# The order in which two engines read a group's score banks, one table for Exp and Ln, and the order of the first and last turns, in a two-layer cross-attention kernel

## The chip, the cores and the metric

The kernel runs on one core of a Trainium2 chip, entirely in fp32. The metric is the device time of one execution in microseconds (us), as the median of several executions. The engines are named as in the profile: PE (matrix multiplies), DVE (VectorE), ACT (ScalarE), POOL (GpSimd), and SP, whose queue issues nearly all the DMAs. "L77" is line 77 of the kernel.

## The reference, cut to what matters

Two cross-attention layers follow each other on x of 4 x 512 x 320; both read the same context of 4 x 1024 x 512, and both have 20 heads of 16 and four image tokens ("ip") at the end of the context. Layer 0 also fuses a second score into the ip attention: the text probabilities times the *context itself* (512 columns), normalised to length one and multiplied with the normalised ip tokens.

```python
def layer0(x, ctx):
    text, ip = ctx[:, :-4], ctx[:, -4:]
    probs = softmax(q @ k_text.T * D**-0.5)                      # per head, 512 x 1020
    text_out = probs @ v_text
    qsem = l2norm(probs @ text)                                  # per head, 512 x 512
    sem = qsem @ l2norm(ip).T
    probs_ip = softmax(q @ k_ip.T * D**-0.5 + 0.5 * sem) * spatial_mask
    return (text_out + probs_ip @ v_ip) @ W_out + b_out + x

def layer1(x, ctx):
    text, ip = ctx[:, :77], ctx[:, 77:]                          # ip: the other 947 rows
    out = softmax(q @ k_text.T * D**-0.5) @ v_text + softmax(q @ k_ip.T * D**-0.5) @ v_ip
    return out @ Wo.T + bo + x
```

## The kernel before, in words

**Work and loops.** A turn is one batch and one block of 128 queries: 16 turns. A turn has five groups of four heads, so there are 80 groups `gi` in one long loop, and each group is two `Unit`s (pairs of heads). A `Unit` has four parts (`part0` to `part3`), in which PE makes layer 0's large products of probabilities and context (tiles named `b`). After every part comes a `stop`, numbered k = 0 to 7 within the group. A stop takes one item from a queue (`sub`, else `late`, else `proj`, which holds the next batch's projections), then does what the loop's rules add to it:

```python
        item()
        if k < 2:
            fill0(gi + 1, k)
        if k in (2, 4, 5, 6) or ending[0] and k < 2 or gi >= len(G) - HG and k == 7:
            l1_step()
```

**The scores of the next group.** `fill0(gi + 1, k)` calls `fill` (L464), for the context half c = k. PE writes 32 small products `sc` into two PSUM tiles of two banks each, two heads to a tile; the heads alternate, so that the first two products need tile 0 and the third already needs tile 1. For each tile in turn, ACT copies it to `e` (L476) and DVE takes the maximum over the blocks of the half (`m`, L477; the profile gives it the line of the helper, L87). The tiles come from the pool `ps_sc`, which holds just two of them. The next half's `sc` therefore take the same two tiles, and so do layer 1's score products: `mx` (scores for the maximum, in `do_max`) and `ex` (the same scores less the maximum, for Exp, in `do_exp`).

**Layer 1.** It runs one turn late, in `l1_step`s. A step makes `mx` of group g + 1, takes the rows' maxima on DVE, and then makes `ex` of group g, whose Exp is on ACT. After four steps of a group, `do_pv` multiplies with the values, and `normalise` divides on DVE and POOL. A turn is `linked` if at least four steps of the turn before are still queued: its maxima then ride on those steps, instead of having two steps of their own (`first_maxima`).

**The end of a turn of layer 0.** `finish(turn)` (L831) is emitted after the turn's fifth group. It works on small tiles of 128 x 20 to 128 x 320: the reciprocal of the sums, the squared lengths `n2`, a `Sqrt` on ACT (L857) and a reciprocal for 1/length, then the ip softmax with an `Exp` on ACT (L866) and the spatial mask. These are the scheduler's to place. Two empty items, `turn_ip`, `add_ip`, `turn_out` and `multiply` follow in the queue `late`, and `multiply` starts layer 1 of the turn.

**Order.** `mm`, `tr` and `vec` keep PE's instructions and those of DVE issued through `vec` in program order; the plain `nc.vector` operations of `finish`, and ACT, POOL and most DMAs, are ordered by a scheduler. [...]

**PSUM.** `ps_sc` has 2 x 2 banks, `ps_qs` three single banks for the `b` products, and `ps_tp` one bank (`tp`) for transposes, projections and `pv`. When the large products are not running (`idle`), `tp` also hands out the three `qs` banks.

**Start and end of the program.** At the start the context of batch 0 is transposed in four quarters (`turns`, tiles `cT`); behind each quarter's transposes come `sums`, DVE combinations of the raw context that are sent to DRAM (`td`) for later products. Then come keys (`keys0`, `last_k`), queries (`q0`) and values (`v0`), whose weights `load_w` brings through two buffers. At the end, after the last group, a loop takes an item and a layer-1 step by turns until nothing is left; there turn 15's layer 0 is finished, and its whole layer 1 runs.

Of the kernel before, what the change touches and what calls it, by code (L numbers as in the profile page):

```python
# [13 lines left out]
F32 = mybir.dt.float32  # L14
AF = mybir.ActivationFunctionType
# [40 lines left out]
def xattn_pair(ctx_stack: ExitStack, tc: tile.TileContext, a: dict, out: bass.AP):  # L56
    nc = tc.nc

    def pool(name, bufs, **kw):
        return ctx_stack.enter_context(tc.tile_pool(name=name, bufs=bufs, **kw))  # L60

    cst = pool("cst", 1)
    big = pool("big", 1)
    wts = pool("wts", 2)
    ep = pool("ep", 8)
    e1p = pool("e1p", 6)
    st2 = pool("st2", 2)
# [25 lines left out]

    ending = [False]
    idle = [True]
    turn_of = [0]

    def tp(name):
        turn_of[0] += 1
        if idle[0] and turn_of[0] % 4:  # L100
            return ps_qs.tile([P, 512], F32, tag=f"qs{turn_of[0] % 4 - 1}", name=name)
        return ps_tp.tile([P, 512], F32, tag="tp", name=name)
# [8 lines left out]
            nc.scalar.copy(o, i)  # L111


    ident = cst.tile([P, P], F32, name="ident")
    make_identity(nc, ident)

# [28 lines left out]
    recent = []  # L145

    def load_w(b, *names):

        for k, t in recent:
            if k == (b, names):  # L150
                return t
        t = wts.tile([P, EC, C + NIP], F32, tag="w", name=f"{'_'.join(names)}_{b}_{len(recent)}_{turn_of[0]}")
# [8 lines left out]
        recent.append(((b, names), t))  # L161
        del recent[:-2]
        return t


# [42 lines left out]
    def normalised_ip():  # L208
        ipraw = st2.tile([B * NIP, E], F32, tag="pc", name="ipraw")
        for b in range(B):  # L210
            nc.scalar.dma_start(ipraw[b * NIP : (b + 1) * NIP, :], a["ctx_2048"][b, NTXT0:T, :])
        ipsq = st2.tile([B * NIP, E], F32, tag="pc", name="ipsq")
        ipn = cst.tile([B * NIP, 1], F32, name="ipn")
        nc.scalar.activation(ipsq, ipraw, AF.Square, accum_out=ipn)
        nc.vector.tensor_scalar(ipn, ipn, EPS2, None, ALU.max)
        ipl = cst.tile([B * NIP, 1], F32, name="ipl")
        nc.scalar.activation(ipl, ipn, AF.Sqrt)
        ipr = cst.tile([B * NIP, 1], F32, name="ipr")
        nc.vector.reciprocal(ipr, ipl)
        nc.vector.tensor_scalar(ipsq, ipraw, ipr, None, ALU.mult)  # L220
        pt = tp("pt_ipn")
        for e in range(EC):
            tr(pt[:, e * 16 : (e + 1) * 16], ipsq[:, e * P : (e + 1) * P], ident[:16, :16])
        nc.vector.tensor_copy(ipnT.rearrange("p e n -> p (e n)"), pt[:, 0 : EC * 16])
# [50 lines left out]
    def projections(b):  # L275
# [9 lines left out]
        z.loads = []  # L285

        def quarter(n):

# [130 lines left out]
            return [[lambda: turn(0), lambda: (turn(1), sums())], [lambda: keys(0)], [last_keys],  # L419
                    [lambda: values0(0), lambda: values0(1)], [values_ip] if n == 3 else [], [lambda: keys(1)], v1]  # L420

        def query_steps(s):
# [41 lines left out]
    def fill(c, m, name):  # L464


        ps = [ps_sc.tile([P, 2, 512], F32, tag="sc", name=f"sc{name}_{c}_{i}") for i in range(2)]
        for j in range(TH):
            t = (TH * c + j) * P
            for r in range(4):  # L470
                mm(ps[r // 2][:, r % 2, j * P : (j + 1) * P], kq[0][0][32 * r : 32 * r + D, t : t + P],
                   qq[0][0][32 * r : 32 * r + D, :], True, True)
        e = []
        for i in range(2):
            e.append(ep.tile([P, 2, TH, P], F32, tag="e0", name=f"e{name}_{c}_{i}"))
            nc.scalar.copy(e[i].rearrange("p h t s -> p (h t s)"), ps[i].rearrange("p h n -> p (h n)"))  # L476
            vec.tensor_reduce(m[:, c, 2 * i : 2 * i + 2, :],  # L477
                                    ps[i][:, :, 0 : (TH - c) * P].rearrange("p h (t s) -> p h s t", s=P), AX.X, ALU.max)
        return e


# [1 line left out]
    def layer1(turn):  # L483
# [5 lines left out]
        def name_of(g):  # L489
            return f"1_{turn}_{g}"  # L490

        def do_max(g, i, half):

            if g not in ms:
                ms[g] = st2.tile([P, 2, 4], F32, tag="m1", name=f"m{name_of(g)}")
            k, m = buffer(1, turn, g), ms[g][:, :, 2 * i : 2 * i + 2]
            ps = ps_sc.tile([P, 2, 512], F32, tag="sc", name=f"mx{name_of(g)}_{i}_{half}")
            for j in range(2):
                r = 32 * (2 * i + j)
                mm(ps[:, j, :], qq[1][k][r : r + D, :], kq[1][k][r : r + D, half * 512 : half * 512 + 512], True, True)  # L500
# [4 lines left out]
            if half == 0:  # L505
                vec.tensor_reduce(rows(R_TXT), ps[:, :, 0:NTXT1], AX.X, ALU.max, negate=True)
            vec.tensor_reduce(m[:, half, :], ps[:, :, 0 if half else NTXT1 : 512], AX.X, ALU.max, negate=True)
            if half:
                vec.tensor_tensor(rows(R_IP), m[:, 0, :], m[:, 1, :], ALU.min)

        def do_sub(g):

            k = buffer(1, turn, g)
            pt = tp(f"pt_nm{name_of(g)}")
            tr(pt[:, 0:P], nmz[k], ident)
            qas[g] = st2.tile([P, P], F32, tag="qa", name=f"qa{name_of(g)}")
            vec.tensor_tensor(qas[g], pt[:, 0:P], qq[1][k], ALU.add)
# [78 lines left out]
        def step(g, k):  # L596
# [8 lines left out]
            nxt = after(1)  # L605
            if nxt and (g + 1 < HG or nxt[0].linked):
                nxt[0].do_max(nxt[1], 1 - x, half)
            if sub:
                sub.popleft()()
            do_exp(g, x, half)  # L610
# [220 lines left out]
    def finish(turn):  # L831
# [6 lines left out]
        def wide(t, n=NIP):  # L838
            return t.unsqueeze(2).to_broadcast([P, H, n])
# [5 lines left out]
        nc.vector.reciprocal(r, pv[:, :, V0W - 1])  # L845
        o = small("o", [P, H, D])
        nc.vector.tensor_tensor(o, pv[:, :, 0:D], wide(r, D), ALU.mult)
        sem = small("sem", [P, H, NIP])
        nc.vector.tensor_tensor(sem, pv[:, :, D : D + NIP], wide(r), ALU.mult)

        n2 = small("n2", [P, H])
        nc.vector.tensor_tensor(n2, ss[:, :, 0], ss[:, :, 1], ALU.add)
        nc.vector.tensor_tensor(n2, n2, r, ALU.mult)
        nc.vector.tensor_tensor(n2, n2, r, ALU.mult)
        nc.vector.tensor_scalar(n2, n2, EPS2, None, ALU.max)
        n1 = small("n1", [P, H])
        nc.scalar.activation(n1, n2, AF.Sqrt)  # L857
        rn = small("rn", [P, H])
        nc.vector.reciprocal(rn, n1)
        nc.vector.tensor_tensor(sem, sem, wide(rn), ALU.mult)  # L860
        pe = small("pe", [P, H, NIP])
        nc.vector.scalar_tensor_tensor(pe, sem, SEM_SCALE, ips, ALU.mult, ALU.add)
        mx = small("mx", [P, H])
        nc.vector.tensor_reduce(mx, pe, AX.X, ALU.max)
        nc.vector.tensor_tensor(pe, pe, wide(mx), ALU.subtract)
        nc.scalar.activation(pe, pe, AF.Exp)  # L866
        sums = small("sums", [P, H])
        nc.vector.tensor_reduce(sums, pe, AX.X, ALU.add)
        re = small("re", [P, H])
        nc.vector.reciprocal(re, sums)  # L870
        nc.vector.tensor_scalar(re, re, spat[:, s : s + 1], None, ALU.mult)
        nc.vector.tensor_tensor(pe, pe, wide(re), ALU.mult)
        of2, box = o.rearrange("p h d -> p (h d)"), {}

        def turn_ip():
# [22 lines left out]
            vec.tensor_tensor(xr[:, 0, :], pt[:, 0:C], xr[:, 0, :], ALU.add)  # L898
            layer1(turn)


        late.extend([lambda: None] * 2 + [turn_ip, add_ip, turn_out, multiply])


    z, (turns, keys0, last_k, v0, vip, keys1, v1, q0) = projections(0)
# [12 lines left out]

    run(keys0[3:])
    load_w(0, "L0_xattn_W_k", "L1_xattn_Wk")  # L920
    run(keys0[:3])
    run(q0[:4])
    run(last_k)
    load_quad(0, z, 0, 0)
    run(v0[:2])
    load_w(0, "L0_xattn_W_v_ip")
# [57 lines left out]
    for gi, (turn, g) in enumerate(G):  # L984
# [49 lines left out]
```

## Time and profile before

| what | value |
|---|---|
| median of 3 runs (lowest, highest) | 3739.45 us (3739.18, 3739.75) |
| the profiled execution's own time | 3740.82 us |
| its span | 3739.0 us |
| mean granted PE clock | 0.961 |
| busy: PE, DVE, ACT, POOL | 94%, 56%, 40%, 27% |
| PE busy in the first 100 us, and from 3600 us to the end | 65.77 of 100.00; 89.32 of 139.00 |

The span is the time between the first and the last recorded instruction; the execution's time is 1.8 us longer. PEclk is the share of full clock that PE was granted. The row of a group of instructions gives busy time and the mean of one; the idle time of that engine just before them stands behind, with what ended it.

### The profile page before, as it was taken

What the parts mean: (1) busy time and instruction counts of PE and PEld (TensorE: products, weight loads), DVE (VectorE), ACT (ScalarE), POOL (GpSimd) and SP (SyncE); (2) the same over time, 40 slices, a digit from 0 to 9 for tenths busy, and PEclk for the clock granted to TensorE, in tenths of its full rate; (3) what the DMA queues carried; (4) which work ended last, traced back from release to release, by engine and by line L of the source; (5) the groups of instructions that cost most, each with busy time, mean ns of one, the idle gap of its engine ahead of it and who ended that gap; (6) DMA issues with size and microseconds to landing.
All of it is one profiled execution on the core that took longest, in us unless ns stands there. A gap on an engine that the chain in (4) does not pass through costs nothing.

```text
span 3739.0 us, 74161 instructions
## 1 busy us (share of the span) xinstructions
PE 3529.3 (94%) x29060; PEld 2812.8 (75%) x29060; DVE 2083.0 (56%) x3794; ACT 1500.1 (40%) x2824; POOL 1015.8 (27%) x1040
## 2 busy tenths in 40 slices
PE   6999999999999999999999999999999999999976
PEld 5777777777788777877777787777777777777765
DVE  2344555665655654666564555556656666665543
ACT  1333344444443433444443433444444444444432
POOL 2222222322232222232232222223223323322210
PEclk8999999999999999999999999999999999999986
DMA  6354332222344243222324334222232222222211
GB/s 193 103 133 113 89 72 39 43 40 53 78 95 114 59 98 87 53 51 42 70 65 111 90 90 100 46 58 40 48 82 44 43 44 51 41 46 38 45 35 26
DMA packets 704987, 258.76 MB, mean 69 GB/s; under 512 B 571024, under 2 KB 679024, under 8 KB 704640
## 3 DMA queue, kind: packets, MB, share of 16 engines
q1 hardware_dynamic: 704464, 253.82, 30.1%
q8 instruction: 232, 3.80, 0.4%
q14 instruction: 115, 0.94, 0.1%
q10 hardware_dynamic: 176, 0.20, 0.0%
HBM read 213.51 MB, written 40.33 MB: 68 GB/s over the span
## 4 chain that ended last, share of the span: by engine, by line
PE 80%; DVE 11%; ACT 3%; issue 2%; DMA 2%; SPq 1%; POOL 0%; ACTq 0%; POOLq 0%; DVEq 0%
PE b L77 48%; PE ex L77 6%; PE pv L77 5%; DVE m L87 4%; PE sc L77 4%; PE pt_k L77 4%; DVE e L87 4%; PE mx L77 4%; PE pt_v L77 4%; PE pt_y L77 2%; PE pt_q L77 2%; PE mx L92 1%; ACT e L710 1%; ACT e L476 1%; ACT junk L790 1%
## 5 line engine op out<-in xcount | busy, mean ns | idle before, releaser
L77 PE MATMUL b<-xv_t,e 128*128 128x277 f32 x2560 | 669.8, 404 | 0.5 <-DVE c L87 0.4
L77 PE MATMUL b<-xv,e 128*128 128x277 f32 (+1 forms) x2560 | 652.6, 407 | 2.7 <-ACT e L710 2.7
L77 PEld LDWEIGHTS b<-xv,e 128*128 128x128 f32 x2560 | 479.4, 190 | 136.9 <-ACT e L710 3.2
L77 PEld LDWEIGHTS b<-xv_t,e 128*128 128x128 f32 x2560 | 482.2, 193 | 113.6 <-DVE c L87 3.1
L710 ACT ACTIVATE e<-e 128x1024 f32<-128x1024 f32 x320 | 338.3, 1057 | 456.0 <-DVE e L87 455.7
L805 POOL TENSOR_TENSOR e<-e,s 128x512 f32<-128x512 f32 x160 | 224.2, 1401 | 1081.1 <-PE b L77 1081.1
L87 DVE TENSOR_REDUCE m<-sc 128x256 f32<-128x1024 f32 (+1 forms) x320 | 338.1, 1088 | 282.9 <-ACT e L476 282.9
L529 ACT ACTIVATE e<-ex 128x1024 f32<-128x1024 f32 x320 | 326.0, 1019 | 236.7 <-PE ex L77 236.6
L87 DVE TENSOR_REDUCE m<-mx 128x2 f32<-128x870 f32 (+1 forms) x320 | 363.8, 1137 | 96.9 <-PE ex L77 90.6
L790 ACT ACTIVATE junk<-c 128x256 f32<-128x256 f32 x480 | 198.7, 414 | 486.4 <-DVE c L87 478.5
L77 PE MATMUL ex<-qa,kq 19*128 19x128 f32 x5120 | 383.3, 290 | 6.8 <-DVE qa L87 5.9
L77 PE MATMUL mx<-kq,qq 16*128 16x512 f32 x1280 | 365.3, 661 | 21.5 <-DVE m L87 15.6
L476 ACT COPY e<-sc 128x1024 f32<-128x1024 f32 x320 | 307.5, 1012 | 193.5 <-PE sc L77 192.3
L87 DVE TENSOR_TENSOR e<-e,bc 128x1024 f32<-128x1024 f32 x320 | 368.4, 1172 | 2.1 <-DMA bc<-zd 2.1
L712 POOL TENSOR_TENSOR e<-e 128x512 f32<-128x512 f32 x160 | 206.4, 1290 | 577.1 <-ACT e L710 577.1
L87 DVE TENSOR_TENSOR c<-b,p 128x256 f32<-128x256 f32 x320 | 134.2, 419 | 405.1 <-PE b L77 359.1
L77 PE MATMUL b<-xs,e 128*128 128x256 f32 x1280 | 359.8, 430 | 0.0
L77 PEld LDWEIGHTS ex<-qa,kq 19*128 19x128 f32 x5120 | 321.5, 192 | 12.6 <-DVE qa L87 5.4
L77 PE MATMUL b<-xs_t,e 128*128 128x256 f32 x1280 | 319.8, 393 | 5.9 <-POOL e L805 5.9
L77 PE MATMUL b<-xs_t,s 128*128 128x256 f32 x1280 | 302.6, 379 | 1.3 <-ACT p L804 1.3
L77 PE MATMUL sc<-qq,kq 16*128 16x128 f32 x5120 | 219.1, 298 | 87.4 <-DVE m L87 87.4
L77 PEld LDWEIGHTS b<-xs,e 128*128 128x128 f32 x1280 | 255.3, 209 | 54.8 <-issue 4.1
(190 smaller groups left out, 4223.6 us busy)
## 6 DMA issues: line engine op xcount, KB each, us to landing
kq<-kd SPq DMA_DIRECT2D x640, 64.0 KB
v1q<-v1d SPq DMA_DIRECT2D x80, 373.5 KB
bc<-zd SPq DMA_DIRECT2D x80, 256.0 KB
xv<-v0d SPq DMA_DIRECT2D x480, 42.0 KB
xv_t<-v0d SPq DMA_DIRECT2D x320, 42.0 KB
L_xattn_W_k<-in_L_xattn_W_k_dram SPq DMA_DIRECT2D x13, 640.0 KB
L_xattn_W_v<-in_L_xattn_W_v_dram SPq DMA_DIRECT2D x13, 640.0 KB
raw<-in_ctx_dram SPq DMA_DIRECT2D x32, 256.0 KB
```

The lines of the kernel that those rows point to most:

```text
L77: tc.keep_in_program_order(nc.tensor.matmul(out, lhsT=lhsT, rhs=rhs, start=start, stop=stop, skip_group_check=on))
L87: return lambda *args, **kw: keep(getattr(self.engine, name)(*args, **kw))
L92: tc.keep_in_program_order(nc.tensor.transpose(out, in_, ident))
L476: nc.scalar.copy(e[i].rearrange("p h t s -> p (h t s)"), ps[i].rearrange("p h n -> p (h n)"))
L529: nc.scalar.activation(e.rearrange("p i j s -> p (i j s)"), ps.rearrange("p i n -> p (i n)"), AF.Exp)
L710: nc.scalar.activation(flat, flat, AF.Exp)
L712: nc.gpsimd.tensor_tensor(e[:, 1], e[:, 1], e[:, 0], ALU.subtract)
L790: nc.scalar.activation(junk, x, AF.Square, accum_out=self.w["ss"][:, self.h + r, k : k + 1])
L805: nc.gpsimd.tensor_tensor(self.e("11"), self.e("11"), self.s2, ALU.add)
```

## The change

- **`fill`**: for the second tile (i = 1), the DVE maximum is emitted ahead of the ACT copy; for the first it stays behind it.
- **One table**: at the start ACT is told to load one set of functions (number 6). Square roots are gone; 1/length is Exp(-0.5 Ln(n2)).
- **`finish`** is in three pieces, all through `vec`: `norms` at once, `exps` and `shares` as the first two items of `late` (where the empty ones were), so ahead of the two fills of the new turn's second group.
- **Stops**: in the last five groups, no layer-1 step at k = 7 any more, and none at k = 6 in the last two.
- **The tail**: a flag `tail` is set after the last group. From then on `do_max` takes two single banks of `ps_qs` for each tile instead of one `sc` tile, with a DVE reduction for each bank; the transposes of `do_sub` (`pt_nm`) take them too, and `tp` gives only its own bank. A waiting `pv` is emitted between `mx` and `ex` of a group's first step. First the queue `late` is emptied, with layer-1 steps beside it while more than five are left; then the old loop runs.
- **The start**: batch 0's `sums` come behind the transposes of all quarters, each in front of a quarter's keys; `last_k` and `q0` interleave differently, and the load of `L0_xattn_W_v` is issued in front of two of the `last_k`. `load_w` names its two buffers as slots and keeps two at a time as before.

```diff
     wts = pool("wts", 2)   ->   wts = pool("wts", 1)         # tags w0 and w1
+    def tail_bank(name):
+        bank_of[0] += 1
+        return ps_qs.tile([P, 512], F32, tag=f"qs{bank_of[0] % 3}", name=name)
 def tp(name):
+        if tail[0]:
+            return ps_tp.tile([P, 512], F32, tag="tp", name=name)
+    nc.scalar.add_instruction(mybir.InstLoadActFuncSet(name=nc.get_next_instruction_name(), act_func_set_id=6))
...
-        nc.scalar.activation(ipl, ipn, AF.Sqrt)
-        nc.vector.reciprocal(ipr, ipl)
+        nc.scalar.activation(ipr, ipn, AF.Ln)
+        nc.scalar.activation(ipr, ipr, AF.Exp, scale=-0.5)
...
 def fill(c, m, name):
-            nc.scalar.copy(e[i].rearrange("p h t s -> p (h t s)"), ps[i].rearrange("p h n -> p (h n)"))
-            vec.tensor_reduce(m[:, c, 2 * i : 2 * i + 2, :],
-                                    ps[i][:, :, 0 : (TH - c) * P].rearrange("p h (t s) -> p h s t", s=P), AX.X, ALU.max)
+            read = [lambda: nc.scalar.copy(e[i].rearrange("p h t s -> p (h t s)"), ps[i].rearrange("p h n -> p (h n)")),
+                    lambda: vec.tensor_reduce(m[:, c, 2 * i : 2 * i + 2, :],
+                                              ps[i][:, :, 0 : (TH - c) * P].rearrange("p h (t s) -> p h s t", s=P), AX.X,
+                                              ALU.max)]
+            for f in read[::-1] if i else read:
+                f()
...
 def do_max(g, i, half):
-            ps = ps_sc.tile([P, 2, 512], F32, tag="sc", name=f"mx{name_of(g)}_{i}_{half}")
+            if tail[0]:
+                ps = [tail_bank(f"mx{name_of(g)}_{i}_{half}_{j}").unsqueeze(1) for j in range(2)]
+            else:
+                ps = [ps_sc.tile([P, 2, 512], F32, tag="sc", name=f"mx{name_of(g)}_{i}_{half}")]
...
+            for j, p in enumerate(ps):
+                mine = slice(j * n, j * n + n)
+                if half == 0:
+                    vec.tensor_reduce(rows(R_TXT)[:, mine], p[:, :, 0:NTXT1], AX.X, ALU.max, negate=True)
+                vec.tensor_reduce(m[:, half, mine], p[:, :, 0 if half else NTXT1 : 512], AX.X, ALU.max, negate=True)
 def do_sub(g):
-            pt = tp(f"pt_nm{name_of(g)}")
+            pt = (tail_bank if tail[0] else tp)(f"pt_nm{name_of(g)}")
 def step(g, k):
+            if tail[0] and k == 0 and pend:
+                pend.pop()()
...
 def finish(turn):
+        def norms():
+            vec.reciprocal(r, pv[:, :, V0W - 1])
+            vec.tensor_tensor(n2, ss[:, :, 0], ss[:, :, 1], ALU.add)
+            vec.tensor_tensor(n2, n2, r, ALU.mult)
+            vec.tensor_tensor(n2, n2, r, ALU.mult)
+            vec.tensor_scalar(n2, n2, EPS2, None, ALU.max)
+            nc.scalar.activation(rn, n2, AF.Ln)
+            nc.scalar.activation(rn, rn, AF.Exp, scale=-0.5)
+            vec.tensor_tensor(o, pv[:, :, 0:D], wide(r, D), ALU.mult)
+            vec.tensor_tensor(sem, pv[:, :, D : D + NIP], wide(r), ALU.mult)
+        def exps():
+            vec.tensor_tensor(sem, sem, wide(rn), ALU.mult)
+            vec.scalar_tensor_tensor(pe, sem, SEM_SCALE, ips, ALU.mult, ALU.add)
+            vec.tensor_reduce(mx, pe, AX.X, ALU.max)
+            vec.tensor_tensor(pe, pe, wide(mx), ALU.subtract)
+            nc.scalar.activation(pe, pe, AF.Exp)
+        def shares():
+            vec.tensor_reduce(sums, pe, AX.X, ALU.add)
+            vec.reciprocal(re, sums)
+            vec.tensor_scalar(re, re, spat[:, s : s + 1], None, ALU.mult)
+            vec.tensor_tensor(pe, pe, wide(re), ALU.mult)
-        late.extend([lambda: None] * 2 + [turn_ip, add_ip, turn_out, multiply])
+        norms()
+        late.extend([exps, shares, turn_ip, add_ip, turn_out, multiply])
...
-    run(keys0[:3])
-    run(q0[:4])
-    run(last_k)
+    for i in range(3):
+        z.sums[i]()
+        keys0[i]()
+    z.sums[3]()
+    run(q0[:2])
+    run(last_k[:1])
+    run(q0[2:4])
+    run(last_k[3:])
+    load_w(0, "L0_xattn_W_v", slot=0)
+    run(last_k[1:3])
...
-        if k in (2, 4, 5, 6) or ending[0] and k < 2 or gi >= len(G) - HG and k == 7:
+        if k in (2, 4, 5) or k == 6 and gi < len(G) - 2 or ending[0] and k < 2:
             l1_step()
...
-    idle[0] = True
+    idle[0] = tail[0] = True
+    while late:
+        item()
+        if len(l1) > 5:
+            l1_step()
+        stops[0] += 1
     while sub or late or l1 or pend:
```

More of the change, by code (lines that the diff above doesn't have):

```diff
@@ L63, in xattn_pair @@
     big = pool("big", 1)
-    wts = pool("wts", 2)
+    wts = pool("wts", 1)
     ep = pool("ep", 8)
@@ L95, in xattn_pair @@
     idle = [True]
+    tail = [False]
     turn_of = [0]
+    bank_of = [0]
+    def tail_bank(name):
+        bank_of[0] += 1
+        return ps_qs.tile([P, 512], F32, tag=f"qs{bank_of[0] % 3}", name=name)
     def tp(name):
         turn_of[0] += 1
+        if tail[0]:
+            return ps_tp.tile([P, 512], F32, tag="tp", name=name)
         if idle[0] and turn_of[0] % 4:
@@ L143, in load_x, with load_w @@
         return t
[L145 to L152, printed above, removed]
+    held = [None, None]
+    newest = [1]
+    def load_w(b, *names, slot=None):
+        for x in held:
+            if x and x[0] == (b, names):
+                return x[1]
+        newest[0] = 1 - newest[0] if slot is None else slot
+        t = wts.tile([P, EC, C + NIP], F32, tag=f"w{newest[0]}", name=f"{'_'.join(names)}_{b}_{turn_of[0]}")
         for i, name in enumerate(names):
@@ L160, in load_w @@
             nc.gpsimd.tensor_copy(t[:, :, C:], ipnT[:, :, b * NIP : (b + 1) * NIP])
-        recent.append(((b, names), t))
-        del recent[:-2]
+        held[newest[0]] = ((b, names), t)
         return t
@@ L215, in normalised_ip @@
         nc.vector.tensor_scalar(ipn, ipn, EPS2, None, ALU.max)
-        ipl = cst.tile([B * NIP, 1], F32, name="ipl")
-        nc.scalar.activation(ipl, ipn, AF.Sqrt)
         ipr = cst.tile([B * NIP, 1], F32, name="ipr")
-        nc.vector.reciprocal(ipr, ipl)
+        nc.scalar.activation(ipr, ipn, AF.Ln)
+        nc.scalar.activation(ipr, ipr, AF.Exp, scale=-0.5)
         nc.vector.tensor_scalar(ipsq, ipraw, ipr, None, ALU.mult)
@@ L284, in projections @@
         z.xr = {}
-        z.loads = []
+        z.loads, z.sums = [], []
         def quarter(n):
@@ L418, in quarter @@
                 v1[0:1] = [lambda: values1_first(0), lambda: values1_first(1)]
-            return [[lambda: turn(0), lambda: (turn(1), sums())], [lambda: keys(0)], [last_keys],
+            z.sums.append(sums)
+            return [[lambda: turn(0), lambda: (turn(1), b and sums())], [lambda: keys(0)], [last_keys],
                     [lambda: values0(0), lambda: values0(1)], [values_ip] if n == 3 else [], [lambda: keys(1)], v1]
@@ L496, in do_max @@
             k, m = buffer(1, turn, g), ms[g][:, :, 2 * i : 2 * i + 2]
-            ps = ps_sc.tile([P, 2, 512], F32, tag="sc", name=f"mx{name_of(g)}_{i}_{half}")
+            if tail[0]:
+                ps = [tail_bank(f"mx{name_of(g)}_{i}_{half}_{j}").unsqueeze(1) for j in range(2)]
+            else:
+                ps = [ps_sc.tile([P, 2, 512], F32, tag="sc", name=f"mx{name_of(g)}_{i}_{half}")]
             for j in range(2):
                 r = 32 * (2 * i + j)
-                mm(ps[:, j, :], qq[1][k][r : r + D, :], kq[1][k][r : r + D, half * 512 : half * 512 + 512], True, True)
+                o = ps[j][:, 0, :] if tail[0] else ps[0][:, j, :]
+                mm(o, qq[1][k][r : r + D, :], kq[1][k][r : r + D, half * 512 : half * 512 + 512], True, True)
             def rows(row):
                 return nmz[k].rearrange("p (r n) -> p r n", r=4)[:, 2 * i : 2 * i + 2, row]
-            if half == 0:
-                vec.tensor_reduce(rows(R_TXT), ps[:, :, 0:NTXT1], AX.X, ALU.max, negate=True)
-            vec.tensor_reduce(m[:, half, :], ps[:, :, 0 if half else NTXT1 : 512], AX.X, ALU.max, negate=True)
+            n = 2 // len(ps)
+            for j, p in enumerate(ps):
[3 more added lines that the diff above has]
+                vec.tensor_reduce(m[:, half, mine], p[:, :, 0 if half else NTXT1 : 512], AX.X, ALU.max, negate=True)
             if half:
@@ L844, in finish @@
         r = small("r", [P, H])
-        nc.vector.reciprocal(r, pv[:, :, V0W - 1])
         o = small("o", [P, H, D])
-        nc.vector.tensor_tensor(o, pv[:, :, 0:D], wide(r, D), ALU.mult)
         sem = small("sem", [P, H, NIP])
-        nc.vector.tensor_tensor(sem, pv[:, :, D : D + NIP], wide(r), ALU.mult)
         n2 = small("n2", [P, H])
-        nc.vector.tensor_tensor(n2, ss[:, :, 0], ss[:, :, 1], ALU.add)
-        nc.vector.tensor_tensor(n2, n2, r, ALU.mult)
-        nc.vector.tensor_tensor(n2, n2, r, ALU.mult)
@@ L855, in finish @@
-        nc.vector.tensor_scalar(n2, n2, EPS2, None, ALU.max)
-        n1 = small("n1", [P, H])
-        nc.scalar.activation(n1, n2, AF.Sqrt)
         rn = small("rn", [P, H])
-        nc.vector.reciprocal(rn, n1)
-        nc.vector.tensor_tensor(sem, sem, wide(rn), ALU.mult)
         pe = small("pe", [P, H, NIP])
-        nc.vector.scalar_tensor_tensor(pe, sem, SEM_SCALE, ips, ALU.mult, ALU.add)
         mx = small("mx", [P, H])
-        nc.vector.tensor_reduce(mx, pe, AX.X, ALU.max)
-        nc.vector.tensor_tensor(pe, pe, wide(mx), ALU.subtract)
@@ L866, in finish @@
-        nc.scalar.activation(pe, pe, AF.Exp)
         sums = small("sums", [P, H])
-        nc.vector.tensor_reduce(sums, pe, AX.X, ALU.add)
         re = small("re", [P, H])
-        nc.vector.reciprocal(re, sums)
-        nc.vector.tensor_scalar(re, re, spat[:, s : s + 1], None, ALU.mult)
-        nc.vector.tensor_tensor(pe, pe, wide(re), ALU.mult)
+        def norms():
[8 more added lines that the diff above has]
+            vec.tensor_tensor(sem, pv[:, :, D : D + NIP], wide(r), ALU.mult)
```

## The prediction

> **What bounds the kernel now.** I read the page first (busy shares, chain), then PE's waits, then the windows by stage, then the timeline around single stalls. Of 3739.0 us PE is busy 3529.3; what can be won or lost is its idle time, about 210 us less the records' rounding, and its clock.
>
> ```profile
> PE 3529.3 (94%) x29060; PEld 2812.8 (75%) x29060; DVE 2083.0 (56%) x3794; ACT 1500.1 (40%) x2824; POOL 1015.8 (27%) x1040
> PE 80%; DVE 11%; ACT 3%; issue 2%; DMA 2%; SPq 1%; POOL 0%; ACTq 0%; POOLq 0%; DVEq 0%
> ```
>
> PE's waits (total, times, longest) and the windows (PE busy, clock behind POOL's busy) say where:
>
> ```profile
> PE sc L77 <- DVE m L87: 87.4, 62, 4.2
> PE pt_v L77 <- DMA L_xattn_W_v<-in_L_xattn_W_v_dram: 16.5, 3, 10.9
> PE mx L77 <- DVE m L87: 15.6, 8, 3.0
> ...
> 0.00:100.00 100.00, 65.77 (x333) 50.65 (x334) 25.55 (x58) 15.24 (x26) 20.38 (x53) 0.84 0.64 191
> 100.00:3500.00 3400.00, 3277.34 (x26742) 2614.29 (x26741) 1950.92 (x3543) 1411.53 (x2680) 958.91 (x946) 0.98 0.31 68
> 3600.00:3650.00 50.00, 31.94 (x290) 22.62 (x288) 15.26 (x39) 9.43 (x14) 3.21 (x5) 0.69 0.12 29
> 3650.00:3700.00 50.00, 31.59 (x391) 27.15 (x387) 22.65 (x36) 12.09 (x14) 2.35 (x4) 0.63 0.14 35
> ```
>
> There are three places: the second half's `sc` waiting for the maxima in the middle (87.4 us), the start, and the tail, with the clock at 0.63 to 0.69. One such stall in the middle (group 63), from the timeline:
>
> ```profile
> 2862.03 1.91 ACT L476 COPY e<-sc 128x1024 f32<-128x1024 f32 x2
> 2863.05 2.36 DVE L87 TENSOR_REDUCE m<-sc 128x256 f32<-128x1024 f32 x2 [1.39 <-ACT e L476]
> 2864.33 0.49 PE L77 MATMUL sc<-qq,kq 16*128 16x128 f32 x4 [1.09 <-DVE m L87]
> 2865.46 1.16 PE L77 MATMUL sc<-qq,kq 16*128 16x128 f32 x28 [0.64 <-DVE m L87]
> 2866.55 3.10 PE L77 MATMUL b<-xs,e 128*128 128x256 f32 x8
> ```
>
> ACT copies tile 0 and then tile 1; DVE reduces tile 0 once its copy ends, then tile 1. PE waits 1.09 for tile 0 and 0.64 for tile 1. Copy 1 runs beside reduce 0 and costs nothing. The eight products after the stall take 3.10 us.
>
> **The change part by part.**
>
> *Reads of the banks.* "Crosswise" would mean that DVE takes tile 1 while ACT takes tile 0. That is not what the edit gives. `vec` keeps program order, and in it reduce 0, which waits for copy 0, still stands in front of reduce 1. Only the order for tile 1 is turned: copy 1 now waits for reduce 1. The chain becomes copy 0, reduce 0, reduce 1, copy 1, all in a row. Tile 0 comes free when it did; tile 1 comes free one copy later (1.01 us by the row of `e<-sc`, 1.05 with the handover). In group 63: 2866.5 instead of 2865.4. I went through all 80 fills: `sc` of the second half stalls already in 31 (15 of them at a finish), and each gets 1.05 more. In 28 more the tile came free only 0.1 us or so ahead of PE, and they get 0.92 to 1.04. In 21 PE arrives late enough for nothing to happen. That is 56.7 us, or 41 us without the finish fills. After the second half, layer 1's `ex` takes the same tile: about 27 times 0.34 us = 9 us. Queued behind the waiting copy 1 on ACT is only `u` or `p`, needed later. Sum +50 us; from +40 (some stalls swallow later ones) to +58.
>
> [...]
>
> *Clock.* After the stall of group 63 the row says x8 in 3.10 us; at full clock those eight take 1.99. The records have the clock at half in stretches of 3.4, 6.8 or 10.2 us, 163.8 us in the middle, so each stretch of 3.4 costs 1.7 us. [...] I take the rows: 11 stalls go from 3.4 to 6.8 (+19 us), and a handful of ungated ones gain one or two stretches (+13): +32 us. [...]
>
> *Finish.* Now, two table loads of 1.28 us each stand in front of the maxima at a finish fill (group 61: `sc` ends 2773.9, copies only at 2778.97, stall 4.19 + 0.43). All 35 loads but one go. Afterwards the chain there is Ln, Exp for the length, 4 DVE operations, Exp, then copies and reductions; `shares` (four of 0.24 to 0.28 us) come behind the reductions. With the durations of that stretch, copy 0 starts at 2777.6 instead of 2778.97 and reduce 1 ends at 2781.0; the serial copy 1 ends at 2782.05, so PE gets its tile at 2782.1 instead of 2782.93. That is 0.8 x 15 = -12 us, the 1.05 of the read order already inside. Bounds -25 (if `norms` also clears the queue for others) and +5. The many table loads elsewhere sat in idle time: 16 of `n` had 0.3 us of idle before them in all.
>
> *Tail.* Before, from the last `b` product (3600.2) to 3739.0 it is 138.8 us. Two loads go from the chain of turn 15's finish: `pt_nm` at 46.5 after the last product instead of 52.7 (-6). Then five groups, at 16.5 us each (3652.9 to 3718.8 for four):
>
> ```profile
> 3679.97 1.23 DVE L87 TENSOR_REDUCE m<-mx 128x2 f32<-128x1024 f32 x1 [2.26 <-PE ex L77]
> 3681.24 1.22 PE L77 MATMUL mx<-kq,qq 16*128 16x512 f32 x2 [1.30 <-DVE m L87]
> 3681.29 1.22 PE L77 MATMUL ex<-qa,kq 19*128 19x128 f32 x8
> 3683.37 1.22 DVE L87 TENSOR_REDUCE m<-mx 128x2 f32<-128x1024 f32 x1 [1.98 <-PE ex L77]
> ```
>
> A step of 3.4 us is `mx` and `ex` together (2.33 at half clock), then 1.30 of waiting, because the next `mx` needs the tile that DVE is reading. With `mx` in its own banks that wait goes, and with it much of the half clock. What is late next is DVE: per group eight bank reductions (0.18 + 0.57 four times, 0.66 four times, interpolated from 0.26 for 154 elements and 1.22 for 1024), `den` 1.75 + 0.44, and small ones, 8.9 us. I take 11 us a group, -5.5 x 4 = -22. About four steps with a `pv` (7.7 us of PE) move from the loop into the tail, where they run beside the finish chain: -7 more. Sum -35; bounds -12 (steps stay at half clock, moved steps delay the chain, `tp` has one bank) and -42.
>
> *Start.* cT copies no longer stand behind `sums` on DVE and a table load goes: keys could begin near 16 instead of 23.75. Against it, the td DMAs of all `sums` stand in SP's queue ahead of the second half of the `L1_xattn_Wk_ip` load, and the xT copy stands behind the last `sums` on DVE. W_v is issued before two `last_k` and not at 64.3, so `pt_v` should start near 59 instead of 69.3 (its wait is the 10.9 above). Value -10; bounds -3 (the weight arrives no earlier) and -16.
>
> *The rest* (Ln in place of Sqrt for 16 tokens, slots for weights) keeps its place in the queues; the weights' order in the middle is as before. Exp from the joint table I cost at nothing, since the elements and not the function set its 1057 ns; were each 5% longer, ACT at 40% would hide it save at the finishes, under 2 us.
>
> Sum: +50 + 32 - 12 - 35 - 10 = **+25 us**. The profiled execution lasted 3740.8 and the median is 1.4 less; the difference is applied to the median: 3739.45 + 25, **3764 us**.
>
> **The rivals.**
>
> *A: the tail and the start win, faster.* If PE's lateness catches most of copy 1 (the 28 near misses disappear as soon as DVE runs a microsecond later everywhere, and new stalls do not gate) the middle costs +25 - 12, and -45 stands against it: -32, about 3708. It decides once the middle costs less than 45. For it: the tail's waits are plain in the rows. Against it: the serial chain is fixed by waits, and the stall repeats with the same numbers in group after group. Chance 0.23.
>
> *B: cancelled.* Middle +55 with a weak clock effect, tail and start at -50: about 3743, no change. What a measurement can tell from no change is about 0.2%, 7.5 us. Chance 0.14.
>
> *C: the clock takes it all, much slower.* Every stall of 1 us and more gates, middle +110, and the tail gives only -15 because its steps remain at half clock: +85, 3825. It decides from the point where 1 us stalls gate in most fills. For it: stalls of 1.73 already do. Against it: only one stretch in the trace follows a stall as short as 0.64. Chance 0.13.
>
> **How the numbers follow.** The main case (slower, 3748 to 3795, most likely 3764) has 0.50. C adds 0.13: slower 0.63, same 0.14, faster 0.23. The unknown costs of the middle (+35 to +105) and of start and tail (-15 to -58) bound the main case; to leave out only 2 in 10 I go from 3710, most of A, to 3805, a part of C.
>
> **What would show it.** On ACT the second copy of a fill should no longer overlap the first: two rows with idle released by `m`. PE's wait `sc` <- should be near 130 us and be released by ACT `e` for a large part, no longer by `m` alone; half clock in the middle near 230 us. At a finish stall no ACT_TABLE_LOAD, about 4.3 us. In the tail steps without the 1.30 wait, groups near 11 us, and the last `b` product at about 3653 (3600 + 70 - 10 - 7). `pt_v` near 59. I am wrong if reduce 1 is seen running beside copy 0, if `sc` waits stay under 90 us, or if the stalls have longer gaps but no more half clock.

## The result, and the profile after

The changed kernel takes 3790.93 us (median of 4 runs, 3787.54 to 3793.58) against 3739.6 us: slower, with a ratio of 1.0134 (95% interval 1.0116 to 1.0151), or +51 us. The sign and the mechanism in the middle were as forecast; the size was twice the forecast +25, because the gain that the tail was to bring did not come.

The page of the changed kernel, its busy shares and its chain:

```profile
PE 3571.5 (94%) x29060; PEld 2848.1 (75%) x29060; DVE 2094.3 (55%) x3814; ACT 1470.5 (39%) x2807; POOL 1015.1 (27%) x1040
PE 77%; DVE 12%; ACT 5%; issue 2%; DMA 2%; SPq 1%; POOL 0%; ACTq 0%; POOLq 0%; DVEq 0%
```

PE does the same 29060 instructions, and is yet busy 42 us longer; by the account below 32 of these are time at half clock, and 10 are not. PE's waits (total, times, longest), then windows (PE busy first, clock behind POOL's busy):

```profile
PE sc L77 <- ACT e L488: 67.9, 55, 1.7
PE sc L77 <- DVE m L87: 56.9, 31, 3.4
PE pt_nm L92 <- DVE nmz L87: 13.5, 7, 3.9
...
0.00:100.00 100.00, 68.59 (x343) 54.01 (x344) 25.06 (x58) 14.60 (x27) 17.51 (x50) 0.88 0.63 186
100.00:3500.00 3400.00, 3247.91 (x26284) 2597.88 (x26283) 1923.50 (x3468) 1360.23 (x2616) 945.40 (x936) 0.97 0.30 68
3650.00:3700.00 50.00, 36.50 (x362) 25.86 (x360) 23.28 (x62) 11.24 (x17) 3.21 (x5) 0.64 0.13 32
3700.00:3750.00 50.00, 44.88 (x469) 32.41 (x469) 23.78 (x54) 12.38 (x15) 3.53 (x6) 0.60 0.18 43
```

A releaser that did not exist before, ACT `e`, now holds `sc` back 55 times. In the tail PE is busy 45 of 50 us, at a clock of 0.60. The stall of group 63 in the changed kernel, from its timeline:

```profile
2905.03 0.99 ACT L488 COPY e<-sc 128x1024 f32<-128x1024 f32 x1
2906.05 2.35 DVE L87 TENSOR_REDUCE m<-sc 128x256 f32<-128x1024 f32 x2 [1.39 <-ACT e L488]
2907.33 0.49 PE L77 MATMUL sc<-qq,kq 16*128 16x128 f32 x4 [1.09 <-DVE m L87]
2908.50 1.01 ACT L488 COPY e<-sc 128x1024 f32<-128x1024 f32 x1 [2.48 <-DVE m L87]
2909.56 2.08 PE L77 MATMUL sc<-qq,kq 16*128 16x128 f32 x28 [1.74 <-ACT e L488]
2911.57 3.78 PE L77 MATMUL b<-xs,e 128*128 128x256 f32 x8
```

ACT is idle for 2.48 us before the second copy, which now stands behind both maxima, and PE waits 1.09 + 1.74 instead of 1.09 + 0.64. The eight rows of `b` take 3.78 us instead of 3.10. (A row of PE is one pass, and a product here is two: `sc` has 5120 rows in 160 fills, so 32 rows for the 16 products of a fill, and the four rows ahead of the second wait are the two products that need tile 0 alone.)

**An account by stage.** For each trace I cut the span at the first scores of group 1 and at the end of the last `b` product, and split PE's time by its records and the trace's clock records, which are at 1.00 or at 0.50 in all 86 of the kernel before and all 96 of the changed one: idle; busy at half clock; and *full work*, the busy time less half of what was busy at half clock. So a stage lasts idle + full work + half of its time at half clock. All in us:

| kernel | start | middle: length = idle, half clock, full work | tail: length = idle, half clock, full work |
|---|---|---|---|
| before | 118.7 | 3481.6 = 122.7, 153.5, 3282.2 | 138.7 = 49.7, 63.2, 57.4 |
| changed | 115.1 | 3535.4 = 153.2, 205.0, 3279.7 | 137.6 = 28.0, 82.4, 68.5 |

The loss in the span, +49.1, is start -3.6, middle +53.8 (idle +30.5, half clock +25.7, work -2.5) and tail -1.1. The forecast, cut in the same way, was -10, +63 (the moved steps taken out) and -28.

Other kernels below have the same start or the same tail, and show how far one trace can be trusted. Starts of the old order took 116.7 to 118.7 us in four traces, those of the changed order (`x_early` left out) 113.8 to 118.9 in nine: -3.6 is within that spread. The changed tail took 134.1 to 138.3 us in four traces, the old one 136.2 to 143.7.

The clock records also show what follows a single stall. In the kernel before, 11 of the 15 stalls of 1.09 + 0.64 us were followed within 7 us by a half-clock stretch of 3.4 us, and 4 by none. In the changed kernel, of the 16 stalls of 2.83 us outside a finish 15 were followed by 6.8 us and one by 3.4; of the 24 new ones of 0.54 to 0.69 us only one was followed by any.

### The profile page after: what moved, and what is told of

Read it like the earlier page. It is cut to its first block, busy times and chain, and to the rows that moved or that the text cites. A ratio compares the mean times of both kernels' runs of the same rounds, so it can differ in the third digit from the quotient of the medians.

```text
span 3788.1 us, 74202 instructions
## 1 busy us (share of the span) xinstructions
PE 3571.5 (94%) x29060; PEld 2848.1 (75%) x29060; DVE 2094.3 (55%) x3814; ACT 1470.5 (39%) x2807; POOL 1015.1 (27%) x1040
## 4 chain that ended last, share of the span: by engine, by line
PE 77%; DVE 12%; ACT 5%; issue 2%; DMA 2%; SPq 1%; POOL 0%; ACTq 0%; POOLq 0%; DVEq 0%
PE b L77 46%; PE ex L77 6%; DVE m L87 5%; PE pv L77 5%; PE sc L77 4%; DVE e L87 4%; PE mx L77 4%; PE pt_k L77 4%; PE pt_v L77 3%; ACT e L488 3%; PE pt_y L77 2%; PE mx L92 1%; PE pt_q L77 1%; ACT e L735 1%; ACT junk L815 1%
## 5 line engine op out<-in xcount | busy, mean ns | idle before, releaser
L735 ACT ACTIVATE e<-e 128x1024 f32<-128x1024 f32 x320 | 338.3, 1057 | 463.2 <-DVE e L87 463.1
L488 ACT COPY e<-sc 128x1024 f32<-128x1024 f32 x320 | 323.1, 1010 | 481.9 <-DVE m L87 351.3
L87 DVE TENSOR_REDUCE m<-mx 128x2 f32<-128x870 f32 (+3 forms) x345 | 366.9, 1066 | 91.5 <-PE ex L77 75.9
L77 PE MATMUL mx<-kq,qq 16*128 16x512 f32 x1280 | 374.6, 659 | 4.7 <-DVE m L87 2.6
L77 PE MATMUL b<-xs,e 128*128 128x256 f32 x1280 | 372.1, 441 | 0.0
L77 PE MATMUL sc<-qq,kq 16*128 16x128 f32 x5120 | 241.7, 309 | 125.2 <-ACT e L488 67.9
L77 PEld LDWEIGHTS sc<-qq,kq 16*128 16x128 f32 x5120 | 196.8, 206 | 191.3 <-ACT e L488 79.5
L77 PEld LDWEIGHTS b<-xs,e 128*128 128x128 f32 x1280 | 263.3, 216 | 59.1 <-issue 7.3
```

The source lines that it names most:

```text
L77: tc.keep_in_program_order(nc.tensor.matmul(out, lhsT=lhsT, rhs=rhs, start=start, stop=stop, skip_group_check=on))
L87: return lambda *args, **kw: keep(getattr(self.engine, name)(*args, **kw))
L488: read = [lambda: nc.scalar.copy(e[i].rearrange("p h t s -> p (h t s)"), ps[i].rearrange("p h n -> p (h n)")), lambda: vec.tensor_reduce(m ...
L735: nc.scalar.activation(flat, flat, AF.Exp)
```

## The experiments

The ratios are to the kernel before, which was measured again beside each set of kernels: 3741.26 us for experiments 1 to 3 and the tail's order, 3740.91 for the first dummy kernels, the tail without its banks and the start, 3738.81 for the rest.

**1. The turned order alone.** The kernel before with the fill's edit only.

```diff
-            nc.scalar.copy(e[i] ...); vec.tensor_reduce(m ...)          # for i in 0, 1
+            for f in read[::-1] if i else read:
+                f()
```

> The kernel before with only the order of the two reads of the second score tile turned (DVE maximum ahead of ACT copy). Theory (serial chain: the second tile comes free one copy later, and the longer stalls also hold PE's clock at half for longer): the middle loses 57 us in the fills, 9 us in front of layer 1's ex and about 25 to 30 us through the clock, so 3739 becomes about 3830 (3805 to 3850), and ACT's second copy of a fill no longer overlaps the first. Rival 1 (only the waits count, the clock does not): about 3805. Rival 2 (the loss of the changed kernel is elsewhere, in its finish, start or tail): 3740 to 3760.

Measured 3821.67 us, ratio 1.0217 (1.0200 to 1.0234). Its waits:

```profile
PE sc L77 <- DVE m L87: 69.4, 31, 4.2
PE sc L77 <- ACT e L476: 67.1, 54, 1.7
```

Waits of `sc` 136.5 instead of 87.4; in the middle idle +46.9, half clock +53.1 us of busy time, which is 26.6 of length, and full work +7.7, which this account does not explain; the middle is 81 us longer. The turned order alone loses more than the whole change. Both rivals are out.

**2. The changed kernel with the old order.**

```diff
-            for f in read[::-1] if i else read: f()
+            nc.scalar.copy(e[i] ...); vec.tensor_reduce(m ...)
```

> The changed kernel with the old order of the two reads, all else kept. Theory: the read order alone makes the loss; without it the finish (-12 or better), the start (-3.6 by the two traces) and the tail (-12 by the two traces) remain: about 3712 (3700 to 3722), faster than the kernel before. Rival (one table and the finish in pieces are themselves a loss): 3740 or more.

Measured 3692.88 us, ratio 0.9874 (0.9860 to 0.9889): 98 better than the changed kernel and better than forecast. Its middle is 3442.4 = idle 104.0, half clock 130.0, work 3273.4. The 15 stalls at a finish add up to 47.2 us where the kernel before has 60.0, and the shorter stalls bring 11.8 us of clock with them. So with the old order everything else in the change is a gain of some 47 us. The parts do not simply add: +80 for the turned order and -47 for the rest would make +33, and the change is +51. On top of the turned order the rest leaves the middle's half clock as it was (206.6 in experiment 1, 205.0 in the changed kernel), where with the old order it takes it from 153.5 to 130.0.

**3. Really crossed.**

```diff
+        copy(0)
+        most(1)      # the maximum of tile 1, on DVE
+        most(0)
+        copy(1)
```

> The changed kernel with the reads really crossed: DVE takes the maximum of tile 1 while ACT copies tile 0, then they change over. Theory: both tiles come free after two rounds of about 1.2 us; the stall of 1.73 becomes about 1.0, that of a finish about 4.0, near misses stay covered: 3690 to 3705, some 10 to 20 better than with the old order. Rival (ACT and DVE slow each other in the score banks, or the second half's first products need tile 0 at the old time and nothing is won): as with the old order, about 3712.

Measured 3617.45 us, ratio 0.9670 (0.9656 to 0.9685): far past what either side expected. Group 63, from its timeline:

```profile
2786.63 1.22 DVE L87 TENSOR_REDUCE m<-sc 128x256 f32<-128x1024 f32 x1
2787.08 1.91 ACT L488 COPY e<-sc 128x1024 f32<-128x1024 f32 x2
2788.10 1.23 DVE L87 TENSOR_REDUCE m<-sc 128x256 f32<-128x1024 f32 x1 [0.25 <-ACT e L488]
2789.04 1.51 PE L77 MATMUL sc<-qq,kq 16*128 16x128 f32 x32 [0.74 <-ACT e L488]
```

DVE starts on tile 1 before ACT starts on tile 0, and one wait of 0.74 is left. The middle is 3364.5 = idle 75.4, half clock 62.1, work 3258.1. Against experiment 2 that is -28.6 idle, -34 through the clock and -15 of full work which this account does not explain. The stall of 1.73 us, expected to become about 1.0, is 0.74, and the clock came on top. The clock records show why it did: 16 stalls of 0.74 us are left outside a finish, and none of them is followed by half clock, where 10 of the 16 stalls of 1.73 us in experiment 2 are. The copy (1.01 us) and the maximum (1.22) are within 1% of what they take alone in the kernel before: in different banks the two engines do not slow each other here.

**4. Dummy work in the stalls: is it the clock?** The kernel before, with products that nobody reads in the 31 stalls.

```diff
+        busy(keep[0], o)            # before the second half's sc; n per group from the trace; o: spare columns of a bank
         mm(ps[r // 2] ...)          # sc
+                if j == 0 and r == 1:
+                    busy(keep[1], o)
```

> The kernel before (old read order), to which dummy PE products are added that nobody reads, just ahead of the second half's sc and between its first two and its third product, only in the 31 groups that stall there, as many as fit into the stall seen in the trace (4 + 2 of about 0.24 us for a stall of 1.09 + 0.64, 17 + 1 for one of 4.19). The scores become ready no earlier, but PE does not stand still. Theory (stalls as short as 1.7 us put the clock at half for 3.4 to 6.8 us): half clock in the middle falls from 164 us to under 40, worth 55 to 75 us: 3665 to 3685. [...]

Measured 3773.47 us, ratio 1.0089 (1.0072 to 1.0106): not the theory's number. Half clock did fall, to 55.1 us, and idle to 72.4, but the work rose by 135 us: a dummy product is two passes (174 products of the next kernel are 348 rows), twice as long as I had sized it, and far more was added than the stalls could take. The next kernel has fewer:

> As clock_fillers, with two faults of it mended: each dummy product is two PE passes of 0.21 us and so twice as long as it was sized, and in the finish fills it waited for a DVE read of its bank. Now 2 + 1 products of 0.42 us stand in a stall of 1.09 + 0.64 and 9 + 1 in one of 4.19 + 0.4, in the idle bank of the transposes at a finish. Theory: dummy work just fills the idle time, idle + dummy stay at the kernel before's 118 us, and busy time at half clock falls from 153 to about 50, worth 45 to 55 us: 3685 to 3700. Rival (the clock falls for another reason, or the fillers delay as much as they save): 3730 to 3750.

Measured 3692.74 us, ratio 0.9873 (0.9859 to 0.9888). Its groups of `sc` and of the dummies (busy, mean ns of one | idle):

```profile
L77 PE MATMUL sc<-qq,kq 16*128 16x128 f32 x5120 | 204.0, 285 | 18.0 <-DVE m L87 16.0
L77 PE MATMUL busy<-wo,ident 128*128 128x224 f32 x254 | 54.2, 358 | 0.0
L77 PE MATMUL b<-wo,ident 128*128 128x224 f32 x94 | 24.7, 370 | 0.0
```

79 us of useless work, and the kernel is 46 us faster. Middle: idle 57.3 (-65), work 3359.1 (+77), half clock 27.8 (-126, worth 63). Idle and dummy work nearly cancel; the gain is the clock. So the 31 stalls of 1.4 to 4.8 us, 87 us of waiting, cost the kernel before some 63 us more in clock.

**5. The tail: what bounds it.** First the banks were taken away again, with every order kept.

```diff
-            if tail[0]:
-                ps = [tail_bank(...) for j in range(2)]     # mx
+                ps = [ps_sc.tile([P, 2, 512], F32, tag="sc", ...)]
-            pt = (tail_bank if tail[0] else tp)(f"pt_nm{name_of(g)}")
+            pt = tp(f"pt_nm{name_of(g)}")
```

> The changed kernel without its tail's banks: mx and pt_nm take the places that they had before (mx one sc tile with one reduction for both banks, pt_nm and the rest the idle qs banks), all orders kept. Theory (the banks took the 1.30 us waits of mx out, about 20 of them, and half clock gave most of it back): 5 to 12 us slower than the changed kernel, 3796 to 3803. Rival 1 (the banks bring what was forecast, 20 us, and something else in the tail got worse): 3810. Rival 2 (the banks bring nothing, or twice the number of reductions costs what they bring): 3790 or below.

Measured 3801.62 us, ratio 1.0158 (1.0143 to 1.0173); tail 145.5. The banks bring about 8 us by the tails of the two traces (11 by the medians), not 20. But the waits of `mx` for `m` do not come back without them: they are 2.3 us in this tail, and idle time is 25.3. What grows is full work, 68.5 to 76.0, and half clock, 82.4 to 88.2. So the theory's number came out and its reason did not: with the orders kept, the waits of 1.30 us stay away without the banks.

Next, dummy work at `pt_nm`, in the changed kernel; then a third of it.

```diff
+            if tail[0]:
+                for _ in range(7):       # 3 in the second kernel
+                    mm(pt[:, P : 3 * P], ident, wo0[:, 0, 0 : 2 * P], True, True)
             tr(pt[:, 0:P], nmz[k], ident)
+            # and two more behind it in the first kernel
```

> The changed kernel with dummy PE products around each pt_nm of the tail (7 before, 2 behind), in the bank of pt_nm itself, where PE waits 1.66 us for the maxima and then for the sums; nothing else is moved. Theory (the tail stayed at its length because PE runs its groups at half clock, and the gap at pt_nm keeps it there): busy time at half clock falls from 82 us to about 40, the tail from 138 to about 115, total 3765 to 3775. Rival (the tail is bound by DVE and its chain of maxima, the clock only follows): no gain, 3788 to 3795.

> As tail_fillers with a third of its dummy work: 3 products of about 0.5 us ahead of each pt_nm of the tail, which fit into its wait of 1.66 us, none behind. In tail_fillers half clock fell by 37 us of busy time while 30 us of dummy work were added. Theory (clock): dummy work and idle cancel, half clock falls by 20 to 37 us, worth 10 to 18 us: 3773 to 3781. Rival (fewer dummies do not hold the clock, or DVE bounds the group): 3787 to 3795.

The first: 3791.69 us, 1.0136 (1.0121 to 1.0151). Half clock falls from 82.4 to 45.6 as expected, but the dummies add 30 us of work; nothing is won. The second: 3779.96 us, 1.0107 (1.0090 to 1.0125), with tail 127.5 = idle 19.3, half clock 56.6, work 80.0. There 11.5 us of dummies cover 8.7 of idle, and 25.8 less at half clock are worth 12.9. DVE's work is unchanged and the tail is 10 us shorter, so DVE did not bound these groups.

Last, the gap itself was removed: the transpose goes behind the products that do not need it.

```diff
     def item():
-        for q in (sub, late, proj):
+        for q in (late, proj) if tail[0] else (sub, late, proj):
```

> The changed kernel, in whose tail the transpose pt_nm no longer stands in front of a group's first step but behind its mx and pv products, so that PE does not stand still for the maxima (1.66 us in each of six groups). Theory (PE in the tail is bound by its half clock, and these waits keep it there): with the waits gone the clock recovers, groups go from about 15 us to 10, tail 20 to 30 us shorter: about 3765. Rival 1 (only the waits count): 6 x 1.7 = 10 us, about 3780. Rival 2 (DVE bounds the group at 8.9 us plus its own waits, so that a new wait for m comes in its place): within 4 us of 3790.

Measured 3777.47 us, 1.0098 (1.0083 to 1.0113): 13.5 below the changed kernel. A group's head in its timeline:

```profile
3741.17 3.48 PE L77 MATMUL pv<-e,v1q 128*32 128x128 f32 x72
3744.59 0.33 PE L92 MATMUL pt_nm<-ident,nmz 128*128 128x128 f32 x1
3745.30 1.16 PE L77 MATMUL ex<-qa,kq 19*128 19x128 f32 x18 [0.38 <-DVE qa L87]
```

The wait of 1.66 ahead of `pt_nm` is gone and 0.38 behind it is left. Tail 124.1 = idle 21.0, half clock 62.6, work 71.8: 7 us of waiting, and 10 of clock. That is a little more than rival 1 and well short of the theory: the clock recovers in part, and what holds the rest at half is open.

**6. The start.** The second block of x is loaded first.

```diff
+    early[0, 2] = load_x(0, 2, 2, e1p, "e1")
-    transposed_x(load_x(b, s, 2, big, "xin"), ...)
+    transposed_x(early.pop((b, s), None) or load_x(b, s, 2, big, "xin"), ...)
```

> The changed kernel, in which the second block of x of batch 0 has a buffer of its own at the start, so that its load is issued among the first and not at 90.8 us behind bc, windows and biases in SP's queue. Theory (the start lost 7.7 of its 11.3 us to PE's wait for this load, 8.7 us): 5 to 9 us faster than the changed kernel, 3782 to 3786. Rival (the scores' bc and the first Exp are as late, and PE waits for them instead): within 3 us of 3791.

Measured 3792.16 us, 1.0135 (1.0120 to 1.0150): no gain. PE's waits in its first 120 us:

```profile
PE pt_k L77 <- DMA L_xattn_Wk<-in_L_xattn_Wk_dram: 9.7, 1, 9.7
PE pt_k L77 <- DMA W_k_L_xattn_Wk_ip<-in_L_xattn_Wk_ip_dram: 8.2, 1, 8.2
```

The wait for x is gone, and later (at 110.5 us) another transfer takes its place, 9.7 us for the weights of layer 1's keys, for which the changed kernel waits 1.3. My rival named the wrong successor, but its number was right.

**7. The best version.** Crossed reads and the tail's order together, then with dummies in the stalls that are left.

```diff
+        copy(0); most(1); most(0); copy(1)
+        for q in (late, proj) if tail[0] else (sub, late, proj):
+        busy(keep[0], o)            # second kernel only: 7, 3 or 1 for 3.17, 1.61 or 0.74 us
```

> Both best parts together: reads really crossed, and pt_nm behind mx and pv in the tail. Theory (the two act in different stretches, so the gains add): 3617.5 - 13.5 = 3604 (3600 to 3610). [...]

> crossed_tail with dummy PE products in the stalls that are left in front of the second half's sc: 7 of 0.42 us where 3.17 us are waited at a finish, 3 for 1.61, 1 for 0.74. Theory: busy time at half clock in the middle falls from 62 us to about 15, worth 20 to 25 us: 3578 to 3588. Rival (what is left of half clock comes from the projections' and other waits): within 5 us of crossed_tail.

Measured 3612.32 us (ratio 0.9659, 0.9643 to 0.9676) and 3585.41 us (0.9590, 0.9576 to 0.9605). The first stands 5 below the crossed kernel and no more: its tail is 129.8 against 135.0, half clock 71.1, so the tail's gain holds only in part, and 5 us is within the spread of the runs. The dummies bring 27 more: half clock in the middle 65.7 to 23.6. The last one is the fastest of all, 153 us below the kernel before.

## Why the prediction was right and where it failed

**The order of the reads: right in kind, too large.** The edit was read as a serial chain, and the chain is in the rows of all 160 fills: copy, two maxima, copy. Fifteen stalls outside a finish went from 1.73 to 2.83 where +1.05 was forecast (a sixteenth moved from group 77 to 78). Two terms were too large. The near misses were priced at 0.92 to 1.04 each; 24 fills now wait 0.54 to 0.69, because PE still makes the first two products (0.49 us) before it needs tile 1. The 9 us in front of `ex` did not come: the changed kernel's waits show 0.6 us of `ex` for ACT in all. Outside the finish the waits of `sc` grew by 32 us where 41 were forecast. (The forecast's own terms, 31 times 1.05 and 28 times 0.92 to 1.04, add up to 58 to 62 and not to 56.7.)

**The clock: right, a little large in sum.** +25.7 us against +32 forecast, and experiment 4 shows that it is the stalls that bring it (126 us less at half clock with dummies in them). The forecast's step from stretches of 3.4 to 6.8 us is in the records: in the kernel before 11 of the 15 stalls of 1.73 us were followed by 3.4, and of the three of 2.62 to 3.00 two by 6.8 and one by 3.4; in the changed kernel 15 of the 16 of 2.83 were followed by 6.8. Behind the 16 short stalls the half-clock stretches grew from 44.2 to 105.4 us in all, worth 31; at the finishes they fell from 95.2 to 88.4. The clock's part in the forecast range of the middle, +35 to +105, is shown by no run; the runs showed +25.7, and +26.6 with the turned order alone.

**The finish: wrong in sign.** I had it as -12 with the turned order inside. A stall at a finish of the changed kernel (group 61):

```profile
2818.43 1.27 POOL L832 TENSOR_TENSOR e<-e,s 128x512 f32<-128x512 f32 x1
2818.61 1.19 DVE L87 SCALAR_TENSOR_TENSOR pe<-sem,ips 128x80 f32<-128x80 f32 x1
2820.38 0.27 ACT L897 ACTIVATE pe<-pe 128x80 f32<-128x80 f32 x1 [1.97 <-DVE pe L87]
2820.56 0.99 ACT L488 COPY e<-sc 128x1024 f32<-128x1024 f32 x1
2822.86 0.49 PE L77 MATMUL sc<-qq,kq 16*128 16x128 f32 x4 [3.40 <-DVE m L87]
2825.09 2.08 PE L77 MATMUL sc<-qq,kq 16*128 16x128 f32 x28 [1.74 <-ACT e L488]
```

and, in the kernel before, the same DVE operation of that group:

```profile
2777.98 0.24 DVE L862 SCALAR_TENSOR_TENSOR pe<-sem,ips 128x80 f32<-128x80 f32 x1
```

The scores end at 2815.77 and the first copy starts 4.79 us later; my schedule by hand had 3.65, the kernel before 5.02. The table loads went (35 of 1.28 us before, one after; the `Exp` of 128 x 1024 takes 1057 ns in both kernels), but DVE's chain for `pe` still sets the start, and one operation in it takes 1.19 us instead of 0.24: most of the difference to my schedule. In the two traces it takes 1.19 in all 16 cases in which it runs beside an operation of POOL (3 before, 13 after) and 0.24 in the other 16; whether POOL is the cause was not tested. The 15 stalls sum to 65.5 us against 60.0 before, +5.5. Without the turned order (experiment 2) they are 47.2: the finish alone is worth -12.8 of waiting, where my sum needed -28.

That the waits of `sc` grew by 37.8 us in all, against the +38 of the first and the third term (+50 and -12), is luck: one was some 17 too large and the other some 17 too small. With the clock a little below its forecast the middle came out at +53.8 against +63, so it is not what made the total too small.

**The tail: the step that failed.** The prediction says that with the wait gone "much of the half clock" goes, that "what is late next is DVE", and takes 11 us a group. The waits went, the half clock did not. The last five `pt_nm` of the changed kernel stand at 3700.43, 3721.57, 3736.56, 3751.76 and 3766.49: 16.5 us apart on average, as before. The four groups between them, split as above:

| kernel | length = idle, half clock, full work |
|---|---|
| before | 65.9 = 22.6, 36.2, 25.2 |
| changed | 66.1 = 8.1, 47.0, 34.4 |
| changed, transpose behind the products (`tail_order`) | 50.7 = 3.2, 22.7, 36.1 |

Idle and full work alone, 8.1 + 34.4 us, are 10.6 us a group: without half clock the forecast of 11 would have been met. The 5.9 more in each group are what the 47.0 us at half clock cost (23.5 in four groups). DVE is busy 8.3 us of the 16.5 and is not what is late. The head of one such group in the changed kernel:

```profile
3736.56 0.45 PE L92 MATMUL pt_nm<-ident,nmz 128*128 128x128 f32 x1 [1.66 <-DVE nmz L87]
3736.94 2.08 PE L77 MATMUL mx<-kq,qq 16*128 16x512 f32 x4
3738.94 3.75 PE L77 MATMUL pv<-e,v1q 128*32 128x128 f32 x72
3742.62 1.16 PE L77 MATMUL ex<-qa,kq 19*128 19x128 f32 x18
```

One gap of 1.4 to 1.7 us ahead of each `pt_nm` is left, which the prediction did not name. Filling it or removing it (experiment 5) shortens the tail by 10 to 14 us, so these gaps keep part of the half clock, by the table about half of it; the rest is open. That steps might stay at half clock stands in the prediction as a bound and in its rival C. The same tail behind another middle had groups of 14.8 us (`copy_first`) and 15.3 (`crossed`), so a part depends on more than the tail.

A second term was put at nothing: the moved steps were to run beside the finish chain. They took 10 us of work from the loop (full work from group 75 to the last `b`: 231.0 to 221.0; its length fell by 9.9), but the tail has 153 more rows of PE, and its full work grew by 11. In the table above, one more `pv` and the output's products fall between the same transposes, and `mx` and `ex`, which in the kernel before run at the same time for 26.9 us of the four groups, overlap for 17.9. The tail and the moved steps were to bring -35; they brought about -11 (-1.1 and -9.9). That is 24 us short.

**The start: mis-sized.** `pt_v` started at 59.29 as forecast (59; 64.1 and 61.8 in experiments 2 and 3), and the scores of group 0 stood 11.3 us earlier. By group 1 only 3.6 were left. The timeline of PE shows two waits that are new or longer:

```profile
41.69 2.73 PE L77 MATMUL pt_k<-cT,W_k_L_xattn_Wk_ip 128*128 128x179 f32 x8 [8.81 <-DMA W_k_L_xattn_Wk_ip<-in_L_xattn_Wk_ip_dram]
94.30 1.51 PE L92 MATMUL pt_xT<-ident,xin 128*128 128x128 f32 x6 [8.69 <-DMA xin<-in_x_dram]
```

The first is the weight behind the `td` DMAs, which had been named and lies ahead of `pt_v`; the second, 3.2 us in the kernel before, took the gain back, and I had costed the stage up to `pt_v` and stopped there. Experiment 6 shows that it is not this one load: with it early, PE waits for the next transfer.

In sum, in the span: start 6 and tail with the moved steps 24 short of the forecast gains, the rest of the middle 6 below its forecast loss: +49 instead of +25.

## What to carry to other kernels

When two engines read two buffers and the order of both engines is fixed by program order, crossing them means turning the order on *both* (75 us faster in experiment 3 than with the old order); turning it for one buffer alone makes one serial chain (80 us slower in experiment 1), and the timeline shows it as idle time in front of the second reader (2.48 us in group 63). When a wait is removed, ask at which clock the engine will then run before shortening the stage (in this tail idle fell by 21.7 us and half clock grew by 19.2): split each stage into idle, busy at half clock and full work, and forecast all three. When the start waits for transfers, follow a gain to the last transfer that PE waits for before counting it.

## What the runs showed of the hardware that was not expected

In the middle of these kernels the half clock that followed a stall grew with its length: after 0.74 us none (16 of 16, experiment 3), after 1.09 + 0.64 us a stretch of 3.4 us in 11 of 15 cases, after 1.09 + 1.74 us one of 6.8 in 15 of 16. By experiment 4 the 31 stalls of the kernel before (87 us) cost some 63 us more through the clock. In one stretch of the tail PE was busy 90% (44.88 of 50 us) at a mean clock of 0.60. Useless products in the gaps made a kernel faster, by 46 us in one and 27 in another, where they fitted into the gap; 662 rows of them in the same 31 stalls, more than fitted, made it 33 us slower. One small DVE operation took 1.19 us beside an operation of POOL (16 cases) and 0.24 otherwise (16). And ACT and DVE read two different pairs of PSUM banks at once with no slowing over 1%: 1.01 and 1.22 us, as alone.
